# Six result buffers, a fetch lead that grows step by step, and 128 blank rows in a fused attention and expert kernel

## The chip, the cores and the metric

The kernel runs on one core of a Trainium2 chip. The metric is the device time of one execution in microseconds. The profile comes from one further execution, recorded instruction by instruction.

## The reference, cut to what matters

The input is an image tensor of 2 x 56 x 56 positions with 256 channels, all in 32-bit floats. Two layers are applied. The first is a neighbourhood attention with windows of 7 x 7. The second is a linear attention over the 3136 positions of each image, followed by a mixture of eight experts, of which each token uses the two with the highest gate value:

```python
x = x + _L0_conv_ref(_gn(x), ...)             # neighbourhood attention
t = _to_tokens(x)
t = t + _L1_attn_ref(_ln_t(t), ...)           # linear attention, a running sum over tokens
t = t + _L1_ffn_ref(_ln_t(t), ...)            # experts

def _L1_ffn_ref(x, gate_w, gate_b, W1, b1, W2, b2):
    probs = softmax(xf @ gate_w + gate_b)
    top2_vals, top2_idx = top_k(probs, 2)
    # for each expert: out += weight * (gelu(xf @ W1 + b1) @ W2 + b2)
```

An expert's matrices are 256 x 512 and 512 x 256. There are 6272 tokens and so 12544 pairs of token and expert.

## The kernel before, in words

**Stages.** Roughly the first third of the span is the first layer. The second layer then goes through the tokens in 13 steps of 256 tokens per image (`NS1 = 13`, the last step has 64). In step `s`, `attention(s)` is the main line of work; beside it run `before(s + 1)`, which prepares the projections of the next step, `route(s - 1)`, which gates the tokens of the step before, and some expert tiles. `together` advances these generators in proportion: each side line has a nominal count of turns (`n_route = 23` for the routing), and a `yield` in a generator ends one turn. After the last attention step comes a pass in which `route(12)` is the main line, and then the tail, in which only expert tiles are left. The program lists instructions in this order for each engine; the framework's own scheduler may still move an instruction within its engine's queue.

**Routing.** `route` computes for every token and each of its two experts a row number in a DRAM table `xs_d`, in which each expert owns a region of rows (DVE, ending with `rowi`, L1293). It then issues up to eight indirect DMAs from POOL (L1299) that scatter the normalized tokens, with their token numbers and gate values, to those rows.

**Expert tiles.** The rows of an expert are worked in tiles. 48 tiles are whole, with 256 rows, and 9 are half, with 128 rows; `order` mixes them, and from tile 41 on half and whole tiles alternate (half: 41, 43, 45, 47, 49, 51, 53, 55 and 56). A tile passes these places:

- `fetch(k)`: SP loads the rows `xg` (L1452) and the expert's weights and biases `wj` (L1461, 1154 KB). The buffers for both lie in pools of four (`FW = 4`): `fw` during the steps, and from the tail on `fw` and a second pool `tw` in turns of four tiles. `ask(k)` in `experts` lists the fetches of all tiles up to a lead, `use.ahead`, beyond the one being worked. The lead is 2 in the steps and 5 from the start of the tail.
- `gather(k)`: DVE takes the tokens' numbers `rowk` and gate values `cws` from the rows (pool `fs`, six buffers), PE transposes the rows (L1492), ACT copies them (L1496).
- `hidden(k)`: PE multiplies by the first matrix into `p_h` (L1507), ACT applies gelu into `hT` (L1514).
- `results(k)`: ACT writes gate value times bias into the result buffer `ye` (L1526, pool `fy`, four buffers of one tile each); PE multiplies by the second matrix into `p_y` (L1532); DVE multiplies by the gate value and adds into `ye` (L1539); POOL issues an indirect DMA with addition into the output for each 128 rows (L1542). Two tiles can hold the same token, so each addition waits until all additions of the tile before have landed:

```python
before_it = added[-1] if added else []
...
waits_for(add, *before_it)
```

**Blank rows.** Before the first fetch that can reach beyond an expert's last token, `blank()` (L1418) writes empty rows behind each of the eight regions from SP (L1427), so that the unused rows of an expert's last tile hold zero gate values.

Of the kernel before, what the change touches and what calls it, by code (L numbers as in the profile page):

```python
# [24 lines left out]
P = 128  # L25
# [24 lines left out]
NF = FF // P  # L50
# [6 lines left out]
SL = 256  # L57
# [9 lines left out]
FW = 4  # L67
# [24 lines left out]
def sure1(s):  # L92
    return max(0, -((NE * (SL - 1) - assigned(s)) // SL))
# [689 lines left out]
def layer1(tc, t, out, x1_d, xs_d, ident, load, K, plain, lx, last_row, lite):  # L783
# [12 lines left out]
    with ExitStack() as whole:  # L796
# [403 lines left out]
        def route(s):  # L1200
# [3 lines left out]
            for b in range(NB):  # L1204
                store = nc.gpsimd.dma_start(
                    out=out[b * L + s * B1 : b * L + s * B1 + W].rearrange("(j p) e -> p j e", p=T),
                    in_=x[:T, b, :nj, :],
# [70 lines left out]
            n = p2.tile([P, NB * NJ + 1, NE], F32, tag="n", name="n")  # L1278
# [15 lines left out]
                rowi[:T, :, :nt], rows, float(NE * RG), float(NE * RG + SL - 1), ALU.add, ALU.min  # L1294
            )
            yield
            for i in range(nt):
                for c in range(2):
                    put = nc.gpsimd.indirect_dma_start(  # L1299
                        out=xs_d[:, :],  # L1300
                        out_offset=bass.IndirectOffsetOnAxis(
                            ap=rowi[:T, c, i : i + 1].bitcast(U32), axis=0
                        ),
                        in_=xs[:T, i, :],
                        in_offset=None,
                    )
                    tc.declare_no_dep(put.ins, group="puts", reason="slots of other tokens")
                    tc.add_to_no_dep_group("puts", put.ins)
                    tc.add_to_no_dep_group(f"puts{s}", put.ins)
                    puts.setdefault(s, []).append(put)  # L1310
                    tc.declare_no_dep(put.ins, group="gets", reason="full tiles are not written again")
                yield
# [105 lines left out]
        def blank():  # L1418
            for e in range(NE):
                row = nc.values_load(  # L1420
                    behind_[0:1, e : e + 1],
                    engines=[mybir.EngineType.SP],
                    min_val=e * RG,
                    max_val=e * RG + NB * L,
                    skip_runtime_bounds_check_because="an expert has at most K.every token",
                )
                put = nc.sync.dma_start(  # L1427
                    out=xs_d[bass.ds(row, SL), :].rearrange("(u p) c -> p u c", p=P), in_=empty
                )
                tc.declare_no_dep(put.ins, group="puts", reason="slots behind the last token")  # L1430
                tc.declare_no_dep(put.ins, group="gets", reason="full tiles are not written again")
                tc.add_to_no_dep_group("puts", put.ins)
                tc.add_to_no_dep_group(f"puts{NS1}", put.ins)
                puts.setdefault(NS1, []).append(put)

        def fetch(k, pool):
            n = parts(k)
            if filled_at(k) == NS1 and NS1 not in puts:
                blank()
            known = "the lists hold rows of the regions and experts alone"  # L1440
            row, exp = (
                nc.values_load(
                    entry[order[k]][0:1, w, order[k] : order[k] + 1],
                    engines=[mybir.EngineType.SP],
                    min_val=0,
                    max_val=top,
                    skip_runtime_bounds_check_because=known,
                )
                for w, top in ((0, NE * RG), (1, NE - 1))
            )  # L1450
            xg = pool.tile([P, SL // P, ROW], F32, tag="xg", name="xg")
            get = nc.sync.dma_start(  # L1452
                out=xg[:, :n], in_=xs_d[bass.ds(row, n * P), :].rearrange("(u p) c -> p u c", p=P)
            )
            tc.add_to_no_dep_group("gets", get.ins)
            for earlier in range(filled_at(k) + 1):
                waits_for(get, *puts[earlier])
            for later in range(filled_at(k) + 1, NS1 + 1):
                tc.declare_no_dep(get.ins, group=f"puts{later}", reason="slots of later steps")
            wj = pool.tile([P, WJ], F32, tag="wj", name="wj")  # L1460
            nc.sync.dma_start(out=wj, in_=t["we"][bass.ds(exp, 1)].rearrange("o p c -> (o p) c"))  # L1461
            fetched[k] = xg, wj
# [97 lines left out]
        use = SimpleNamespace(ahead=2, asked=0, tail=None)  # L1560
        done = [0]

        def ask(k):
            while use.asked < min(k, NP):
                n = use.asked
                fetch(n, use.w if use.tail is None or (n - use.tail) // FW % 2 else tw)
                use.asked += 1

        def experts():
            for k in range(NP):  # L1570
                ask(k + use.ahead + 1)
                if k == 0:
                    made = gather(0, use.x, use.psum)
                    yield
                wj = fetched[k][1]
                hT = yield from hidden(made[0], wj, use.x, use.psum)
                if k + 1 < NP:
                    following = gather(k + 1, use.x, use.psum)
                    yield
                yield from results(k, hT, made, wj, use.x, use.psum)  # L1580
                made = following
                fetched.pop(k)
                done[0] = k + 1
                yield

        run = experts()

        def until(k):
            while done[0] < k:
                if next(run, 0) is None:  # L1590
                    yield

        def together(main, *others):
            going = [[gen, n, 0] for gen, n in others]
            n_main = main[1]
            made = 0
            for made, _ in enumerate(main[0], 1):
                for o in going:
                    while o[2] * n_main < made * o[1] and next(o[0], 0) is None:
                        o[2] += 1  # L1600
            for gen, _, _ in going:
                for _ in gen:
                    pass
            return made
# [4 lines left out]
        for _ in first:  # L1609
# [6 lines left out]
        empty = load(const, "empty1", [P, SL // P, ROW], t["empty"].rearrange("p (u c) -> p u c", u=SL // P))  # L1616
        nc.gpsimd.dma_start(
            out=xs_d[NE * RG : NE * RG + SL, :].rearrange("(u p) c -> p u c", p=P), in_=empty
# [7 lines left out]
        apart1 = const.tile([1, 1], F32, name="apart1")  # L1626
        nc.vector.tensor_reduce(apart1, pf, AX.X, ALU.max)
        nc.vector.tensor_single_scalar(plain, apart1, 0.0, ALU.is_equal)
        n_att, n_route, per_tile = 26, 23, NF + 1 + SL // P
        for s in range(NS1 + 1):  # L1630
            others = []
            if s == 0:
                others.append((beside_it, NT * NG + 1 - given))
            if s + 1 < NS1:
                others.append((before(s + 1) if s else second, n_before))
            if 0 < s < NS1:
                others.append((route(s - 1), n_route))
            upto_k = max(0, (sure1(s - 2) if s > 1 else 0) - use.ahead)
            n = upto_k - done[0]
            if n > 0:  # L1640
                others.append((until(upto_k), n * per_tile))
            if s < NS1:
                got = together((attention(s), n_att), *others)
                n_att = got if s == 0 else n_att
            else:
                together((route(s - 1), n_route), *others)
            if s + 2 < NS1:
                load_x(s + 2)
            if s == 0:
                beside.close()  # L1650
                lite.close()
                fs, fx, fy, fw = (
                    whole.enter_context(tc.tile_pool(name=n, bufs=k, reuse_waits="tile", side="right"))
                    for n, k in (("fs", 6), ("fx", 2), ("fy", 4), ("fw", FW))
                )
                ps_m = steps.enter_context(
                    tc.tile_pool(name="l_mm", bufs=8, space=PSUM, reuse_waits="tile")
                )
                use.x, use.w, use.psum = fx, fw, ps_m
# [7 lines left out]
        with (  # L1667
            tc.tile_pool(name="tw", bufs=FW, reuse_waits="tile") as tw,
            tc.tile_pool(name="t_ps", bufs=8, space=PSUM, reuse_waits="tile") as ps_t,
            tc.tile_pool(name="tx", bufs=3, reuse_waits="tile") as tx,  # L1670
        ):
            use.x, use.psum, use.ahead, use.tail = tx, ps_t, 5, use.asked
            for _ in run:
                pass

# [901 lines left out]
```

## Time and profile before

| | |
|---|---|
| median of 3 runs | 1396.23 us (1392.82 to 1402.47) |
| the profiled execution | 1395.47 us, span 1393.7 us |
| PE busy | 1249.2 us (90% of the span) |
| DVE, ACT, POOL busy | 788.7, 583.6, 469.3 us |
| mean granted TensorE clock | 0.945 |
| additions into the output (L1542) | 105, 1574 ns each on POOL, idle before them 357.9 us |

The span is the time from the first to the last instruction; 1.77 us of the execution lie outside it. Busy time of POOL at an indirect DMA is the time of the instruction, not of the transfer, which lands some microseconds later. A wait is put down to the event that the trace shows last before it.

### The profile page before, as it was taken

To read this page: it belongs to the slowest core of one execution; us is meant where nothing else is said; L and a number is where in the kernel's file an instruction comes from. 1 tells how busy PE (TensorE), PEld (TensorE's weight loads), DVE (VectorE), ACT (ScalarE), POOL (GpSimd) and SP (SyncE) were. 2 spreads that over 40 slices of the span, in tenths; PEclk is the share of its full clock that TensorE was granted. 3 is DMA by queue.
4 is the path that set the end of the run, shared out by engine and by line. 5 is a ranking of instruction groups with operands and counts; after the bars stand their busy time and mean duration, and the time that the engine had idled before them with its cause. 6 is when DMAs were issued, how large, how long until landed. Compare 5 with 4: busy or idle time off the path is not lost.

```text
span 1393.7 us, 29855 instructions
## 1 busy us (share of the span) xinstructions
PE 1249.2 (90%) x11566; PEld 907.3 (65%) x11566; DVE 788.7 (57%) x2680; ACT 583.6 (42%) x1053; POOL 469.3 (34%) x514
## 2 busy tenths in 40 slices
PE   1899889999989996887999999999999999698893
PEld 1567667677755754445576767676777788587783
DVE  6546555465786657757575666666574755341110
ACT  1443444444444242342554454454535454352341
POOL 0222222223341123133161625253534435452333
PEclk9999999999989697977999999999999999999997
DMA  8345443334431011032435536362726366579852
GB/s 288 90 122 152 121 145 112 116 107 120 130 119 41 25 40 48 18 103 66 173 106 154 163 103 181 93 201 74 196 75 177 93 169 187 173 218 342 276 111 31
DMA packets 101292, 183.21 MB, mean 131 GB/s; under 512 B 15587, under 2 KB 84707, under 8 KB 93845
## 3 DMA queue, kind: packets, MB, share of 16 engines
q1 hardware_dynamic: 69108, 128.96, 28.2%
q0 software_dynamic: 28864, 47.21, 14.8%
q10 hardware_dynamic: 3168, 5.05, 1.1%
q8 instruction: 93, 1.52, 0.5%
q14 instruction: 59, 0.48, 0.1%
HBM read 131.76 MB, written 49.39 MB: 130 GB/s over the span
## 4 chain that ended last, share of the span: by engine, by line
PE 43%; DVE 12%; DMA 4%; issue 3%; ACT 2%; POOL 1%; POOLq 0%; ACTq 0%; DVEq 0%; SPq 0%
PE p_y L1532 11%; PE p_h L1507 9%; PE p_qkv L929 8%; PE p_out L1182 4%; DMA out<-ye,rowk 3%; PE cx L1164 2%; PE p_u L951 2%; PE cx L1151 2%; PE p_sum L966 1%; DVE am L1113 1%; PE pt_x L901 1%; PE p_cf L1064 1%; PE pt_g L1492 1%; ACT wide L1054 1%; DMA out<-x_acc 1%
## 5 line engine op out<-in xcount | busy, mean ns | idle before, releaser
L1542 POOL DMA_INDIRECT out<-ye,rowk x105 | 165.3, 1574 | 357.9 <-DVE ye L1539 100.6
L1532 PE MATMUL p_y<-wj,hT 128*128 128x256 f32 x840 | 206.8, 392 | 25.7 <-ACT hT L1514 19.6
L1507 PE MATMUL p_h<-xT_g,wj 128*128 128x256 f32 (+1 forms) x912 | 209.7, 371 | 2.2 <-DVE ye L1539 1.2
L1532 PEld LDWEIGHTS p_y<-wj,hT 128*128 128x128 f32 x840 | 156.4, 195 | 56.3 <-ACT hT L1514 23.8
L394 ACT ACTIVATE ex<-ex 98x1024 f32<-98x1024 f32 x98 | 103.6, 1057 | 196.2 <-DVE ex L388 192.8
L1507 PEld LDWEIGHTS p_h<-xT_g,wj 128*128 128x128 f32 x912 | 155.4, 191 | 27.3 <-issue 6.0
L1514 ACT ACTIVATE hT<-p_h,wj 128x256 f32<-128x256 f32 (+1 forms) x228 | 99.5, 453 | 106.0 <-PE p_h L1507 105.0
L1539 DVE SCALAR_TENSOR_TENSOR ye<-p_y,cws,ye 128x256 f32<-128x256 f32 x105 | 50.4, 480 | 154.8 <-PE p_y L1532 154.7
L388 DVE TENSOR_TENSOR ex<-sc,bias 98x1024 f32<-98x1024 f32 (+1 forms) x112 | 120.1, 1082 | 27.7 <-PE sc L379 24.2
L379 PEld LDWEIGHTS sc<-qb,kc 64*98 64x98 f32 x1568 | 94.5, 168 | 51.1 <-issue 26.1
L379 PE MATMUL sc<-qb,kc 64*98 64x128 f32 x1568 | 118.3, 289 | 4.0 <-DVE am L1113 2.2
L1299 POOL DMA_INDIRECT xs_d<-xs,rowi x100 | 98.2, 982 | 70.2 <-DVE first L1341 31.4
L402 PE MATMUL po<-vw,ex 98*64 98x33 f32 x3136 | 116.3, 229 | 5.0 <-DMA vw<-v_d 2.7
L402 PEld LDWEIGHTS po<-vw,ex 98*64 98x64 f32 x3136 | 104.9, 143 | 22.8 <-ACT ex L394 4.2
L346 POOL TENSOR_TENSOR xo<-xo,xq 128x256 f32<-128x256 f32 x49 | 36.1, 736 | 226.9 <-DVE xo L340 212.2
L1526 ACT ACTIVATE ye<-wj,cws 128x256 f32<-128x256 f32 x105 | 50.2, 507 | 73.7 <-issue 31.1
L1137 POOL TENSOR_TENSOR zc<-z,blk 128x256 f32<-128x256 f32 x48 | 38.9, 923 | 115.0 <-DVE z L1135 107.0
L506 PE MATMUL pvv<-L_wvT,xs 128*112 128x256 f32 x224 | 61.1, 413 | 13.3 <-DVE top L498 13.3
L873 DVE BATCH_NORM_STATS2 st<-x_acc 128x6 f32<-128x256 f32 (+1 forms) x100 | 38.3, 412 | 51.9 <-DMA x_acc<-x_d 51.5
L1113 DVE TENSOR_TENSOR am<-sc,upto 128x512 f32<-128x512 f32 (+1 forms) x100 | 60.9, 670 | 7.3 <-PE sc L1104 7.2
L348 POOL DMA_DIRECT2D x_d<-xo x98 | 56.7, 580 | 16.6 <-POOL xo L346 14.6
L1176 ACT COPY cT<-cx 128x256 f32<-128x256 f32 (+1 forms) x50 | 18.3, 366 | 103.1 <-PE cx L1164 102.9
(261 smaller groups left out, 2150.0 us busy)
## 6 DMA issues: line engine op xcount, KB each, us to landing
wj<-in_we SPq DMA_DIRECT2D x57, 1154.0 KB
vw<-v_d SPq DMA_DIRECT2D x196, 101.1 KB
xg<-xs_d SPq DMA_DIRECT2D x48, 272.0 KB
v_d<-values POOLq DMA_DIRECT2D x28, 231.0 KB, 3.3
xq<-in_x SPq DMA_DIRECT2D x98, 64.0 KB
x_d<-xo POOLq DMA_DIRECT2D x98, 64.0 KB, 3.2
x_acc<-x_d SPq DMA_DIRECT2D x24, 256.0 KB
out<-x_acc POOLq DMA_DIRECT2D x24, 256.0 KB, 5.1
```

Of the source, the lines that this page charges most:

```text
L379: nc.tensor.matmul(at[p][:KN, b, k], lhsT=keys(i, j, k, b, rows, g), rhs=qb[rows, g, :, b, j * QN : (j + 1) * QN], start=True, stop=True,)
L388: nc.vector.tensor_tensor(ex[:KN, of], sc[:KN].rearrange("n p b k h q -> n p b (k h q)"), tables[kind][:KN, g, of].unsqueeze(2).to_broadca ...
L394: nc.scalar.activation(ex[:KN], ex[:KN], AF.Exp)
L402: nc.tensor.matmul(po[b * QN : (b + 1) * QN, hh, :], lhsT=ex[:KN, h // 2, b, k, h % 2, :], rhs=vw[:KN, b, k, hh * (HD + 1) : (hh + 1) * (H ...
L506: nc.tensor.matmul(ps, lhsT=xs[:, b, k, j * TT : (j + 1) * TT], rhs=wv[:, k, :], start=k == 0, stop=k == NG - 1,)
L929: nc.tensor.matmul(ps[:, :, :W], lhsT=w[:, kk, g * P : (g + 1) * P], rhs=xT[:, kk, :, :W], start=kk == 0, stop=kk == NG - 1,)
L1113: nc.vector.tensor_tensor(am[:T, h, :, :, :T].rearrange("p b g t -> p (b g) t"), sc[:T, :, :, :T].rearrange("p b g t -> p (b g) t"), K.upt ...
L1299: put = nc.gpsimd.indirect_dma_start(out=xs_d[:, :], out_offset=bass.IndirectOffsetOnAxis(ap=rowi[:T, c, i : i + 1].bitcast(U32), axis=0), ...
L1507: nc.tensor.matmul(ph, lhsT=w1[:, k, f * P : (f + 1) * P], rhs=xT[:, k, :], start=k == 0, stop=k == NG - 1,)
L1514: nc.scalar.activation(hT[:, f, :], ph, AF.Gelu, bias=b1[:, f : f + 1])
L1532: nc.tensor.matmul(py, lhsT=hT[:, f, u * P : (u + 1) * P], rhs=w2[:, f, :], start=f == 0, stop=f == NF - 1,)
L1542: add = nc.gpsimd.indirect_dma_start(out=out[:, :], out_offset=bass.IndirectOffsetOnAxis(ap=rowk[:, u : u + 1].bitcast(U32), axis=0), in_= ...
```

## The change

Five edits, in four groups:

1. The result pool `fy` has six buffers instead of four, and `fs`, which holds the row numbers and gate values that go with them, eight instead of six.
2. The lead `use.ahead` is not set to 5 when the tail begins. It grows by one at every odd tile of the tail, from 2, until it is 5.
3. `blank()` writes 128 rows behind each expert instead of 256. A last tile with at most 128 rows is a half tile, so no tile reaches further than that.
4. `route` has one more `yield`, between the row numbers and the scatters, and its nominal count of turns is 24 instead of 23.

```diff
@@ route
                 rowi[:T, :, :nt], rows, float(NE * RG), float(NE * RG + SL - 1), ALU.add, ALU.min
             )
             yield
+            yield
             for i in range(nt):
@@ blank
                 put = nc.sync.dma_start(
-                    out=xs_d[bass.ds(row, SL), :].rearrange("(u p) c -> p u c", p=P), in_=empty
+                    out=xs_d[bass.ds(row, P), :], in_=empty[:, 0, :]
                 )
@@ experts
             for k in range(NP):
+                if use.tail is not None and k % 2 and use.ahead < 5:
+                    use.ahead += 1
                 ask(k + use.ahead + 1)
@@ layer1
-        n_att, n_route, per_tile = 26, 23, NF + 1 + SL // P
+        n_att, n_route, per_tile = 26, 24, NF + 1 + SL // P
...
-                    for n, k in (("fs", 6), ("fx", 2), ("fy", 4), ("fw", FW))
+                    for n, k in (("fs", 8), ("fx", 2), ("fy", 6), ("fw", FW))
...
-            use.x, use.psum, use.ahead, use.tail = tx, ps_t, 5, use.asked
+            use.x, use.psum, use.tail = tx, ps_t, use.asked
```

## The prediction

> **What bounds the kernel now.** I read the page's slices first, then the span cut into stretches, then the waits, and last the time line of POOL and the end of the chain. The slices say that PE is full from about 660 us to 1188 us (18.7 to 20.0 us busy in nearly every 20 us). No edit can give much there. The last fifth is different. Cut into stretches (us, then busy time of PE, PEld, DVE, ACT, POOL, then granted clock, DMA share, GB/s):
>
> ```profile
> 1209.00:1221.00 12.00, 1.96 (x9) 1.25 (x8) 0.00 (x0) 1.70 (x5) 3.17 (x3) 0.66 0.58 167
> 1221.00:1257.00 36.00, 36.00 (x177) 30.29 (x176) 16.62 (x106) 16.05 (x35) 18.40 (x14) 0.97 0.82 222
> 1257.00:1300.00 43.00, 36.09 (x176) 30.77 (x174) 5.37 (x27) 12.26 (x31) 10.80 (x7) 0.92 1.01 365
> 1300.00:1335.00 35.00, 32.25 (x167) 27.46 (x168) 5.61 (x29) 14.07 (x39) 13.80 (x9) 0.95 0.81 228
> 1335.00:1373.00 38.00, 37.52 (x210) 32.76 (x208) 6.94 (x33) 15.44 (x43) 15.54 (x11) 1.00 0.34 49
> ```
>
> PE stands for 10 us at 1209, loses 7 and 3 us in the next two stretches that have holes, and the DMA engines are full from 1257 to 1300. The waits of that part name two queues, ACT and POOL:
>
> ```profile
> ACT ye L1526 <- issue: 31.1, 6, 11.4
> ACT ye L1526 <- DMA out<-ye,rowk: 12.7, 6, 7.2
> POOL out L1542 <- DMA out<-ye,rowk: 81.8, 19, 8.5
> ```
>
> "Issue" hides what it was; the time line of POOL shows it:
>
> ```profile
> 1206.81 0.96 POOL L1299 DMA_INDIRECT xs_d<-xs,rowi  x1 [0.30 <-issue]
> 1208.07 1.60 POOL L1542 DMA_INDIRECT out<-ye,rowk  x1 [0.30 <-issue]
> 1209.98 1.57 POOL L1542 DMA_INDIRECT out<-ye,rowk  x1 [0.30 <-issue]
> 1220.07 1.55 POOL L1542 DMA_INDIRECT out<-ye,rowk  x1 [8.52 <-DMA out<-ye,rowk]
> ...
> 1271.70 1.54 POOL L1542 DMA_INDIRECT out<-ye,rowk  x1 [0.30 <-DVE own_e L1479]
> 1281.73 1.54 POOL L1542 DMA_INDIRECT out<-ye,rowk  x1 [8.49 <-DMA out<-ye,rowk]
> ...
> 1338.80 1.54 POOL L1542 DMA_INDIRECT out<-ye,rowk  x1 [3.68 <-DMA out<-ye,rowk]
> 1340.64 1.54 POOL L1542 DMA_INDIRECT out<-ye,rowk  x1 [0.30 <-issue]
> 1345.25 1.54 POOL L1542 DMA_INDIRECT out<-ye,rowk  x1 [3.07 <-DMA out<-ye,rowk]
> 1349.65 1.54 POOL L1542 DMA_INDIRECT out<-ye,rowk  x1 [2.85 <-DMA out<-ye,rowk]
> ```
>
> Counted back from the last tile, 56, the pair at 1208.07 and 1209.98 is tile 32, 1220.07 is 33, 1271.70 is the second of 39, 1281.73 is 40, 1345.25 is the half tile 49. An ACT bias copy of tile 36 (L1526, 1219.30) needs one of four buffers, the one of tile 32, so it started when the additions of 32 had landed, and two gelus of tile 34 stood behind it in ACT's queue; PE needed them. So ACT is stopped by a full set of buffers, and the buffers are full because the additions go tile by tile. This chain of additions also sets the end:
>
> ```profile
> 1373.29 3.75 DMA out<-ye,rowk
> 1377.82 3.54 DMA out<-ye,rowk
> 1382.39 1.26 POOL out L1542
> ```
>
> PE's last product ends near 1372.6; the rest is additions. Undisturbed, a whole tile costs the chain 6.45 us (1338.80 to 1345.25) and a half tile 4.40 us. PE needs 7.35 us for a whole tile (3.46 + 3.45 + 0.44) and about 3.7 us for a half one. A pair is thus 10.85 us of chain against 11.1 us of PE: nearly even. From 1251.18 (tile 37) to 1382.11 (tile 56) the chain took 130.9 us; 11 whole and 8 half tiles undisturbed are 71.0 + 35.2 = 106.2. The excess of 24.7 us is slow landing: steps of 11.3, 11.9, 10.8 us for the whole tiles 38 to 40 and 8.2 for the half tile 41, all while the DMA share was 1.
>
> **What the Trainium skill says.** "DMA: Bandwidth & Descriptors", section "Issuing engines are not separate DMA queues", says that DMAs from SP and POOL run on the same 16 engines and interleave. Its section "SWDGE vs HWDGE vs iDMA" adds that inside an engine the queues of the two kinds are served in turn. The trace agrees: an addition lands in 3.8 us (median after 1335) and in 8.8 us (median from 1257 to 1300, weight fetches going). So an addition should pay for every microsecond in which fetches are under way, whether they come in one burst or in two. "Perfetto Trace Analysis", section "DMA Instruction — SWDGE (GPSIMD)", says that the profiled end of such an instruction is when the descriptors are written, not when data has moved; here 1.54 us of POOL against 3.5 to 10.1 us to landing.
>
> **The change, part by part.**
>
> *Six result buffers.* A bias copy then needs the additions of two tiles earlier, 10.85 us of chain or more. The 10.0 us hole at 1209 goes, and with it the slow clock behind it (12 products in 4.24 us instead of 2.6): PE gains 11.7 us. In the burst it gains again, since holes of 3.5, 1.4 and 2.9 us before `p_y` are of the same kind. But PE is not what ends last. What the chain of additions gets from an earlier PE is only the time in which it waited for results and not for a landing. With 4.6 us from a second addition to the next tile: tile 35 waited 0.5 us (1233.44 against 1228.32 + 4.6), tile 36 1.9 us, tile 37 3.0 us (its results at 1249.9 and four scatters ahead of it). Sum 5.4 us. The four scatters of step 12 (4 x 1.22 us on POOL) stay; they can lie in the 3 us for which POOL waits for a landing, and the rest, 1.9 us, may stay on the chain. Bounds 3.5 and 5.4 us; I take 5.4, because a chain that never runs dry leaves such a gap at every tile. What is late next: the chain itself, from tile 32 to 56.
>
> *Fetch lead.* SP runs nothing but fetches there. Listing a fetch later in the program puts nothing in front of it: the order on SP stays 41, 42, 43 and so on, and what holds a fetch is a buffer (`p_y` of eight tiles before) or an earlier transfer, as the waits of SP in the tail say (up to 10.4 us for `p_y`, 1.7 to 3.1 us for an earlier `wj`). So I cost it at nothing. If the framework does hold the fetches back, the burst of 41 to 46 at 1257 to 1268 is spread; the bytes stay the same and so, by the section on queues, does most of the excess. Bounds: a gain of 12 us (half the excess) and a loss of 3 us (one tile's weights, 1154 KB at 390 GB/s, late once).
>
> *Blank rows.* Eight DMAs of 136 KB instead of 272 KB. SP's issue time (10.02 us for all eight, the register loads included) hardly changes. 1.09 MB less at 372 to 390 GB/s is 2.9 us less of full DMA engines, and the excess was 18.4 us in the 42 us from tile 38 to tile 41's successor, 0.44 per us: 1.3 us off the chain. Bounds 0 and 2.9.
>
> *The turn in route.* With the old count, one routing turn falls on about one attention turn (24 turns in some 66 us), and there are 20 of them; the scatters begin at the 16th, now at the 17th of 21. They come up to 2.7 us later. They issue eight indirect DMAs (0.98 us each), and behind them in POOL's queue stand `zc` (L1137) and the next additions; SP's fetches of the next rows wait for them to land. POOL waited about 5 us for `rowi` before each block (31.4 us in 7 times), which shrinks. PE was full there, and rows fetched at 1045.08 were transposed no earlier than 1058.59, so a delay of 2.7 us is covered by 9 us. At step 12, where attention has only ten turns, most of the routing runs in one piece, so its eight scatters stay ahead of tile 32's addition. I cost it at 0; bounds -3 (a gain) and +3 us.
>
> Sum: 5.4 + 0 + 1.3 + 0 = 6.7 us off the profiled execution's 1395.47, which is 1388.8. That execution lies 0.8 us under the median of the runs, less than their spread, and I add nothing for it.
>
> **Rivals.** *The additions land faster.* If thinner fetching halves the excess, 12.4 us more go: 1395.5 - 6.7 - 12.4 = 1376.4. For it: tiles 42 and 44 landed in about 4 us between two fetches, so gaps in the fetching do help. Against: the order and the buffers of the fetches stay. At most the whole excess goes, and tile 32 is added before the scatters (results at 1198.8, issued at 1208.07: 9.3 us): 1395.5 - 5.4 - 24.7 - 9.3 = 1356.
>
> *Bias copies run further ahead and block ACT* (the slower side). The framework put tile 36's copy ahead of tile 34's gelu while four buffers allowed it. With six it may put a copy three tiles ahead. It then waits for that tile's weights: the copy of 41 ahead of the gelu of 38 (1250.5) would wait for weights issued at 1257.74 and landed near 1262, 11.5 us in which PE stands, with 1.6 us of slow clock after it. The hole at 1209 comes back in the same way, so nothing is won there: 1395.5 + 13.1 - 1.3 = 1407.3. It decides as soon as a copy stands more than two tiles ahead of the gelu behind it. Against it: in the tail every copy stands one tile ahead, tied to its gate values.
>
> **How the numbers follow.** Forecast 0.46, faster landing 0.36, blocked ACT 0.18. The likeliest is 1388.8. Its own range is 1382 to 1394. The range from 1368 to 1406 leaves out the best end of the first rival and the worse half of the second, under 0.2 in all. About 1% (14 us) is what a measurement of this kernel can tell from no change: faster by more takes most of the first rival and a little of the forecast, 0.38; slower by more the worse part of the second, 0.12; the rest is 0.50.
>
> **What would show it.** Right: no hole in PE near 1209; ACT's waits for `ye` well under 43.8 us; PE's last product more than 13 us before the last addition; POOL waiting for a landing before nearly every tile from 32 to 56; additions still near 9 us under full DMA. Wrong: additions near 4 to 5 us in the burst (first rival), ACT waiting for `wj` or again for `ye` (second), or a PE that ends last, which would mean that the chain of additions was never the bound.

## The result, and the profile after

The kernel after takes 1406.9 us in the median of 17 runs (1401.76 to 1414.02), the kernel before 1397.93 us beside it (17 runs). The ratio is 1.0059, with a 95% interval from 1.0044 to 1.0074: slower by some 8 us, where 6.7 us less were forecast. The profiled execution took 1409.65 us (span 1407.9, mean granted clock 0.936), 14.2 us more than the one before. The two profiles thus lie further apart than the medians, and what is read from them is the place of a loss sooner than its exact size. Of the 14.2 us, 7.7 are there when tile 32 is first added (1208.07 before, 1215.79 after); the other 6.5 lie in the chain of additions from there to tile 56 (174.0 and 180.5 us).

From the added `yield` on, line numbers of the kernel after are one higher: L1543 is L1542 of the kernel before. The tail of the kernel after in stretches (columns: us, busy time of PE, PEld, DVE, ACT, POOL, then clock, DMA share, GB/s):

```profile
1217.00:1229.00 12.00, 12.00 (x65) 9.73 (x63) 1.45 (x3) 3.76 (x10) 4.07 (x4) 1.00 0.90 293
1229.00:1265.00 36.00, 34.49 (x167) 29.25 (x165) 15.87 (x105) 15.08 (x31) 15.38 (x12) 1.00 0.60 142
1265.00:1281.00 16.00, 6.34 (x22) 5.12 (x23) 0.86 (x5) 2.23 (x6) 4.81 (x4) 0.68 0.98 347
1281.00:1309.00 28.00, 24.62 (x145) 22.05 (x143) 5.04 (x28) 10.22 (x27) 6.17 (x4) 1.00 1.05 380
```

The hole that stood at 1209 is gone: PE is busy in all 12 us of the first line. A new one stands in the third, 9.7 us of 16, with the clock at 0.68. The waits of that part (1188 to 1408; us in total, how often, the longest) and ScalarE's time line say who made it:

```profile
POOL out L1543 <- DMA out<-ye,rowk: 99.1, 21, 8.7
ACT ye L1527 <- issue: 16.8, 5, 5.1
ACT ye L1527 <- DMA wj<-in_we: 16.5, 1, 16.5
ACT ye L1527 <- DMA out<-ye,rowk: 11.4, 6, 5.4
```

```profile
1257.09 0.59 ACT L1497 COPY xT_g<-pt_g 128x512 f32<-128x512 f32 x1
1274.17 0.51 ACT L1527 ACTIVATE ye<-wj,cws 128x256 f32<-128x256 f32 x1 [16.49 <-DMA wj<-in_we]
1274.59 1.55 ACT L1515 ACTIVATE hT<-p_h,wj 128x256 f32<-128x256 f32 x4
```

The bias copy of tile 41 stands in ScalarE's queue in front of the four gelus of tile 40. In the kernel before the same copy stood there too (1264.55), but waited only 3.66 us, for numbers from VectorE (`own_e`, worked out from the tile's rows). Now it waits for its weights. These are late because SyncE asks for the rows of tile 41 first, and waits 14.1 us for the last scatters to land. The scatters stand on POOL behind the additions of tile 36:

```profile
SPq L1453 <- DMA xs_d<-xs,rowi: 14.1, 1, 14.1
```

```profile
1248.64 1.54 POOL L1543 DMA_INDIRECT out<-ye,rowk  x1 [8.71 <-DMA out<-ye,rowk]
...
1254.98 1.54 POOL L1543 DMA_INDIRECT out<-ye,rowk  x1 [2.95 <-DMA out<-ye,rowk]
1256.83 1.54 POOL L1543 DMA_INDIRECT out<-ye,rowk  x1 [0.30 <-issue]
1258.67 0.94 POOL L1300 DMA_INDIRECT xs_d<-xs,rowi  x1 [0.30 <-issue]
```

But this hole is not what the additions waited for. The first additions of tiles 38 to 41 found their results ready and waited for the tile before to land:

```profile
1275.36 1.54 POOL L1543 DMA_INDIRECT out<-ye,rowk  x1 [8.33 <-DMA out<-ye,rowk]
...
1287.12 1.54 POOL L1543 DMA_INDIRECT out<-ye,rowk  x1 [8.36 <-DMA out<-ye,rowk]
...
1298.24 1.54 POOL L1543 DMA_INDIRECT out<-ye,rowk  x1 [7.73 <-DMA out<-ye,rowk]
...
1309.91 1.54 POOL L1543 DMA_INDIRECT out<-ye,rowk  x1 [8.28 <-DMA out<-ye,rowk]
```

From tile 37 (1263.56) to tile 42 (1317.27) the chain took 53.7 us, 49.5 before. From tile 32 to 37, where the forecast had its gain, it took 47.8 us in place of 43.1. The steps from 35 to 36 and from 36 to 37 did become shorter, by 2.0 and 0.8 us. But the step from 33 to 34 grew from 6.4 to 9.9 us, with a wait of 6.5 us for results from VectorE, and the step from 34 to 35 from 7.0 to 12.1 us, with the wait of 8.71 us for a landing shown above. No run looks into these two. From 42 to 56 the chain took 79.0 us in place of 81.4.

The end is still additions: from 1358.82 the chain that ended last goes from one landing to the next, and the steps are as long as before:

```profile
1380.90 3.73 DMA out<-ye,rowk
1387.22 3.79 DMA out<-ye,rowk
1391.79 3.74 DMA out<-ye,rowk
```

**A loss before the tail.** 7.7 of the 14.2 us are lost before 1200 us, where I had seen nothing to lose. The first scatter of each step on POOL serves as a mark. The first mark stands at 536.86 before and at 540.05 after; in all the traces of this case it lies anywhere from 535.0 to 541.0, so these 3.2 us are not put down to the change. In the kernel before two later marks stand at 708.16 and 769.51, 61.4 us apart; in the kernel after at 710.52 and 777.27, 66.8 us apart. The steps after that take 66 us in both. So the step of 66.8 us is where the change can have lost 5.4 us. Inside that step VectorE's time line of the kernel after holds this:

```profile
725.46 0.16 DVE L862 SCALAR_TENSOR_TENSOR root<-root_a,root 128x4 f32<-128x4 f32 x1
725.65 4.70 DVE L860 TENSOR_TENSOR root_a<-root 128x4 f32<-128x4 f32 x1
730.38 0.16 DVE L861 SCALAR_TENSOR_TENSOR root_a<-root_a,ve 128x4 f32<-128x4 f32 x1
```

An operation on 128 x 4 numbers that takes 0.16 us in the lines around it took 4.70 us. GpSimd at the same time:

```profile
725.82 2.13 POOL L1205 DMA_DIRECT2D out<-x_acc  x2
727.34 2.98 POOL L914 TENSOR_TENSOR x_acc<-x_acc,bo 128x1024 f32<-128x1024 f32 x1
```

The small operation ends at 730.35, GpSimd's addition of a bias row to the residual tile (L914, in `before`) at 730.32. L860 to L862 are the steps of the inverse root for the normalization in `route`; ScalarE's normalization waits for them (4.9 us at 731.62), two gelus stand behind it, and PE is busy for 2.99 us of the 6 from 728 to 734. In the kernel before, the same chain of small operations ends just before GpSimd begins:

```profile
723.76 0.16 DVE L862 SCALAR_TENSOR_TENSOR root<-root_a,root 128x4 f32<-128x4 f32 x1
723.96 0.16 DVE L881 SCALAR_TENSOR_TENSOR nm<-mv,root 128x4 f32<-128x4 f32 x1
```

```profile
724.17 2.13 POOL L1205 DMA_DIRECT2D out<-x_acc  x2
725.69 2.99 POOL L914 TENSOR_TENSOR x_acc<-x_acc,bo 128x1024 f32<-128x1024 f32 x1
```

724.12 against 724.17: a margin of 0.05 us. Unstopped, VectorE's chain takes 2.6 us from its first step (L878) on. In the kernel before it begins 2.66 us before GpSimd's stores, in the kernel after 1.36 us before them. The other traces say the same. In 13 of the traces of this case the addition L914 has its old place. In the four of them with the turn the chain begins between 1.36 us before the stores and 0.51 us after them, and all four show a stop of 4.0 to 4.7 us. In eight of the nine without the turn it begins 2.6 to 2.8 us before them, and there is no stop. The ninth (six buffers without weight fetches in the tail, which differs from the kernel before only in the result buffers until then) has 1.95 us, and L860 is stopped for 4.69 us at 730.22. The step takes 65.2 to 66.8 us in the five with the stop and 61.4 to 63.9 in the eight without. In the list of GpSimd's instructions the turn alone changes the order in this step only: both `zc` products now stand before the first scatter, and three scatters in place of four before the next addition into the output. How this makes the chain and the stores meet was not followed further.

The Trainium skill names a mechanism: "SBUF — State Buffer", section "Who interferes with whom", says that VectorE and GpSimd share one pair of ports to SBUF, that an operation of VectorE with two inputs in SBUF, or one in a mode that uses both ports, contends with a GpSimd operation that reads SBUF, and that whoever is second is blocked until the other's whole instruction is done. The trace agrees that the small operation ends with GpSimd's addition. It does not agree in who is second: VectorE's operation begins, on record, 1.69 us before the addition (725.65 and 727.34), so the block of 4.70 us is longer than the 2.98 us of the addition. It spans the stores in front of it too. The third and fourth groups of runs below test whether the addition is the cause.

### The profile page after: what moved, and what is told of

Same layout as the page of the kernel before. It is cut to its first block, busy times and chain, and to the rows that moved or that the text cites. A ratio compares the mean times of both kernels' runs of the same rounds, so it can differ in the third digit from the quotient of the medians.

```text
span 1407.9 us, 29872 instructions
## 1 busy us (share of the span) xinstructions
PE 1254.3 (89%) x11566; PEld 911.4 (65%) x11566; DVE 789.4 (56%) x2680; ACT 583.1 (41%) x1053; POOL 468.6 (33%) x514
## 4 chain that ended last, share of the span: by engine, by line
PE 41%; DVE 11%; DMA 6%; ACT 2%; issue 2%; POOL 2%; POOLq 0%; ACTq 0%; DVEq 0%
PE p_y L1533 9%; PE p_qkv L929 8%; PE p_h L1508 8%; DMA out<-ye,rowk 6%; PE p_out L1182 4%; PE cx L1164 2%; PE cx L1151 2%; PE p_u L951 2%; PE p_sum L966 1%; PE pt_x L901 1%; DVE am L1113 1%; POOL out L1543 1%; DVE root_a L860 1%; PE p_cf L1064 1%; PE pt_g L1493 1%
## 5 line engine op out<-in xcount | busy, mean ns | idle before, releaser
L1543 POOL DMA_INDIRECT out<-ye,rowk x105 | 165.3, 1574 | 368.1 <-DMA out<-ye,rowk 109.1
L1533 PEld LDWEIGHTS p_y<-wj,hT 128*128 128x128 f32 x840 | 155.4, 194 | 48.7 <-ACT hT L1515 16.5
L1113 DVE TENSOR_TENSOR am<-sc,upto 128x512 f32<-128x512 f32 (+1 forms) x100 | 60.8, 669 | 6.3 <-PE sc L1104 6.3
L1164 PE MATMUL cx<-am,kp 128*32 128x128 f32 (+1 forms) x800 | 54.7, 309 | 4.7 <-DVE am L1113 4.7
```

The lines of the kernel that those rows point to most:

```text
L1113: nc.vector.tensor_tensor(am[:T, h, :, :, :T].rearrange("p b g t -> p (b g) t"), sc[:T, :, :, :T].rearrange("p b g t -> p (b g) t"), K.upt ...
L1164: nc.tensor.matmul(cx[hp, g, :T], lhsT=kp[:T, b, g, hp], rhs=am[:T, h, b, g, :T], start=False, stop=True,)
L1533: nc.tensor.matmul(py, lhsT=hT[:, f, u * P : (u + 1) * P], rhs=w2[:, f, :], start=f == 0, stop=f == NF - 1,)
L1543: add = nc.gpsimd.indirect_dma_start(out=out[:, :], out_offset=bass.IndirectOffsetOnAxis(ap=rowk[:, u : u + 1].bitcast(U32), axis=0), in_= ...
```

## The experiments

The runs were made in four groups on different chips, on which the kernel before took 1444.46, 1398.93, 1399.96 and 1446.5 us. Each ratio is to the kernel before beside it, and across groups only ratios and stretches of single traces are compared.

**Each part alone.** The six buffers:

```diff
-  (("fs", 6), ("fx", 2), ("fy", 4), ("fw", FW))
+  (("fs", 8), ("fx", 2), ("fy", 6), ("fw", FW))
```

> Six result buffers alone (fs 8, fy 6), everything else as before. The instructions stand in the same order on every engine as in the kernel before; only waits of bias copies differ. Theory A (the chain of additions sets the end, PE's hole near 1209 us goes and the chain never runs dry): 3 to 6 us faster. Theory B (the rows of tile 41 wait for the last step's scatters, and these stand in POOL's queue behind the additions of tile 36, so a PE that is 11 us ahead stands later instead, when the bias copy of tile 41 waits for weights in front of tile 40's gelu): within 3 us of before, or up to 7 us slower, with a wait of ACT for wj of over 10 us near 1260 us.

The lead:

```diff
+                if use.tail is not None and k % 2 and use.ahead < 5:
+                    use.ahead += 1
...
-            use.x, use.psum, use.ahead, use.tail = tx, ps_t, 5, use.asked
+            use.x, use.psum, use.tail = tx, ps_t, use.asked
```

> The growing lead alone. The list of instructions and of their waits comes out the same on all engines as before, so both theories expect no difference: within 2 us. It serves as a measure of how far two equal programs differ.

The blank rows:

```diff
-                    out=xs_d[bass.ds(row, SL), :].rearrange("(u p) c -> p u c", p=P), in_=empty
+                    out=xs_d[bass.ds(row, P), :], in_=empty[:, 0, :]
```

> 128 blank rows alone. Theory A: 1 to 3 us faster (2.9 us less of full DMA engines). Theory B: the fetch of tile 41 waits for blank rows in the kernel before (SP's fetch at 1256.9 us, scatters done at 1250.2 us), so it comes about 3 us earlier, but additions set the end: 0 to 3 us faster.

The turn:

```diff
+            yield
...
-        n_att, n_route, per_tile = 26, 23, NF + 1 + SL // P
+        n_att, n_route, per_tile = 26, 24, NF + 1 + SL // P
```

> The extra turn in route alone (count 24). Theory A: no difference, within 3 us. Theory B': the order of ACT, DVE and PE in the steps changes, with bias copies moved ahead of other copies, and one step near 727 us loses some 5 us while ACT waits for nm; the profile of the changed kernel is 5.4 us later there than the one before: 4 to 7 us slower, all of it before 780 us.

| alone | ratio | interval |
|---|---|---|
| six buffers | 1.0028 | 1.0003 to 1.0053 |
| lead | 1.0000 | 0.9976 to 1.0023 |
| 128 blank rows | 0.9985 | 0.9962 to 1.0007 |
| turn | 1.0027 | 1.0007 to 1.0048 |

The sum is +0.0040, against +0.0059 for all together: the two agree within the intervals. The lead does nothing: with it alone the list of instructions on each engine is the same, in the same order. Buffers and turn each cost some 4 us, with intervals that begin at 0.4 and 1.0 us. With the buffers alone no copy on ScalarE waits for weights in the tail, where theory B had asked for over 10 us, and the additions from tile 37 to 42 take 53.3 us all the same. With the turn alone the step from 711 us on took 65.8 us; in the other three 61.8 to 62.4.

**Three edits of the kernel after, and one of the kernel before.** The turn taken out again (the diff just shown, turned round); the bias copies tied behind their own tile's last gelu (`use.gelu`, set in `hidden`); the last step's routing first; and, on the kernel before, no weight fetches in the tail:

```diff
@@ results: tied copies
-                nc.scalar.activation(y[:, u, :], wj[:, WJ - C :], AF.Identity, scale=cws[:, u : u + 1])
+                behind(nc.scalar.activation(y[:, u, :], ...), use.gelu)
@@ the last step: routing first
-                together((route(s - 1), n_route), *others)
+                list(route(s - 1)) + [list(gen) for gen, _ in others]
@@ fetch: no weights in the tail
+            if use.tail is not None:
+                wj = fetched[use.tail - 1][1]
```

> The kernel after with the added turn taken out again (six buffers, the growing lead and 128 blank rows stay). Theory T, the turn's own loss: the turn alone cost 1.0027 and stretched the step from about 711 to 777 us by 4 to 5 us; without it that step takes 61 to 63 us again, and the ratio to the kernel before falls from 1.0059 to 1.0010 to 1.0025 (buffers 1.0028 and blank rows 0.9985 remain). Rival I, the parts hurt each other in the tail and the turn is innocent: the ratio stays at 1.005 to 1.007, and the loss stands behind the mark at 1200 us.

1.0012 (0.9995 to 1.0030), and the step takes 61.9 us: the turn is worth 0.0047 of the 0.0059. Theory T holds.

> The kernel after with one edit: each bias copy stands in ScalarE's queue behind the last gelu of its own tile, so that it can no longer stand in front of gelus of the tile before. Both theories expect the 16 us wait of the bias copy for the weights of tile 41, and TensorE's hole there, to go. Theory C, the serial additions set the end: the first addition of tile 37 to that of tile 56 still takes 130 to 134 us, and the ratio to the kernel before falls by 0.003 at most, to 1.003 to 1.006. Rival A, the blocked ScalarE queue sets the end: the end comes about 10 us earlier than in the kernel after, ratio 0.997 to 1.000.

1.0115 (1.0088 to 1.0143), outside both expectations. The wait for the weights is gone and nothing is won, which speaks against rival A. It does not rule it out by itself, since the edit brings a wait of its own. Tiles 37 to 56 were added in 137.7 us (132.7 in the kernel after), and VectorE now waits for the copies:

```profile
DVE ye L1540 <- PE p_y L1533: 56.9, 25, 6.0
DVE ye L1540 <- ACT ye L1527: 50.7, 9, 8.8
```

The profiled execution (1408.99 us) is near this kernel's shortest, so it does not show where all of the further loss of 0.0056 lies.

> The kernel after with one edit: in the last step the routing runs to its end before the remaining expert work is begun, so the last four scatters stand on GpSimd in front of the additions of tiles 35 and 36. The slots of tile 41 are then asked for some 10 us earlier and the wait for its weights shrinks below 8 us. Theory C (the additions' chain sets the end, from tile 32 on): the chain from 32 to 56 keeps its length of 173 to 181 us and the end comes 0 to 4 us earlier than in the kernel after: ratio 1.003 to 1.006. Rival A (late fetches behind the scatters set the end): 8 to 12 us earlier, ratio 0.997 to 1.000. Third way: TensorE idles while the routing runs alone, and the ratio rises above 1.007.

1.0009 (0.9983 to 1.0035): 0.0050 less than the kernel after, about 7 us. That is more than theory C allowed and at the edge of rival A. The additions from tile 32 to 56 took 170.2 us in place of 180.5. The rows of tile 41 were asked for at 1245.16 in place of 1264.90, and the fetches behind them met other additions. The chain still sets the end, but its length is not fixed, as theory C had it; I take it that it depends on which additions the fetches meet; this run does not show it.

> The kernel before with one edit that leaves work out: the tiles asked for in the tail fetch no weights and use those of the last tile fetched before the tail. Theory C with contention (an addition lands late because weight fetches fill the DMA engines): the first addition of tile 37 to that of tile 56 shrinks from 131 us to 104 to 112 us, the medians of an addition's landing fall to about 4 us, and the ratio is 0.978 to 0.986. Rival N (the additions take this long by themselves, or the engines' pace spaces them): the stretch stays above 122 us and the ratio at 0.990 or above.

0.9865 (0.9843 to 0.9886), some 19 us, just above the range that theory C gave. Tiles 37 to 56 were added in 110.5 us in place of 130.9, so 20.4 us of the excess of 24.7 go with the weight fetches. A part of them may be results that come earlier, since PE now never stands in the stretch shown. The stretch from tile 37 to 42, in the kernel before and in this one:

```profile
1251.18:1300.68 49.50, 41.91 (x205) 35.90 (x203) 6.57 (x31) 15.50 (x40) 13.97 (x9) 0.93 1.01 352
```

```profile
1250.86:1284.44 33.58, 33.58 (x182) 30.05 (x182) 5.90 (x28) 14.78 (x38) 13.96 (x10) 1.00 0.65 138
```

Rival N falls.

**GpSimd's addition out of VectorE's way.** L914 is queued behind the two `zc` products that follow it on POOL, about 5 us later; nothing needs its result before the next step's attention:

```diff
@@ before
-            nc.gpsimd.tensor_tensor(x[:T, :, :nj, :], ..., ALU.add)
+            use.later.append(lambda: nc.gpsimd.tensor_tensor(x[:T, :, :nj, :], ..., ALU.add))
@@ attention, after the zc products
+                while use.later:
+                    behind(use.later.pop()(), use.zc)
```

> The kernel before with one instruction moved: GpSimd's addition of a bias row to the residual tile (x_acc, 128 x 1024, about 2.95 us) is queued behind the two zc products that follow it, some 5 us later. Theory P (that addition, when it meets VectorE's chain of small steps for the inverse root, holds VectorE up for 3.4 to 4.7 us, and with it ScalarE's gelus and TensorE): where the kernel before shows no such stall after 700 us (a run of about 1398 us), the move brings nothing, ratio 0.998 to 1.002; where it shows one in each step from about 770 us on (a run of about 1444 us, steps of 72 to 75 us in place of 66), the steps come down to 66 us and the ratio to 0.965 to 0.975. Rival Q (the stalls are only where a delay shows, not its source): the steps keep their length, ratio 0.997 to 1.003 in both cases; worse than 1.005 if the later place delays the next step.

> The kernel after with the same instruction moved behind the two zc products. Theory P: the stall of 4.7 us that the turn brought to the step at 711 to 777 us goes, that step takes 61 to 63 us, and the ratio to the kernel before falls from 1.0059 to 1.000 to 1.002 where the kernel before runs at about 1398 us; where it runs at about 1444 us, the ratio is 0.967 to 0.977. Rival Q (the turn costs its 4 to 5 us by another order of TensorE's work): the step keeps 65 to 67 us and the ratio stays at 1.004 to 1.007.

The kernel before with the move: 0.9916 (0.9883 to 0.9949). The kernel after with it: 0.9961 (0.9944 to 0.9978), so the move took 0.0098, about 14 us, off the kernel after. In neither trace does a small operation of the chain take over 1.2 us. The step of 66.8 us takes 63.5, and the move is worth more than theory P had said, in both kernels. I had overlooked that the chain was stopped in earlier steps too: in the kernel before for 2.95, 2.34 and 2.22 us at 551, 605 and 660 us. From the mark near 537 us to that near 708 us the two kernels took 171.3 and 170.5 us, with the move 162.1 and 161.3, so 9.2 us come from there in each. In the step after the mark at 708 the kernel after gains 3.2 us more, and the kernel before, which had no stop there, loses 3.0 (61.4 to 64.3 us), which I had not expected and have not explained.

> The kernel before with one edit: in the last step the routing runs to its end before the remaining expert work is begun, so that the last four scatters stand on GpSimd in front of the additions of tiles 35 and 36. In the kernel after the same edit took 0.0050 off the ratio. If late weights for tile 41 and fetches that meet the additions cost the kernel before as well: 0.994 to 0.998. If it only mends what the six buffers and the turn had brought: 0.999 to 1.002.

> The kernel before with the six buffers (rowk, cws and own_e eight) and with the routing of the last step first. Compared with the routing alone (run beside it). Theory W (six buffers cost 0.003 because the bias copy of tile 41 now stands in ScalarE's queue waiting for weights that come late): with the slots asked for earlier that wait is under 5 us, and the two kernels differ by less than 0.0015, or the buffers win. Rival V (the buffers' cost lies elsewhere): this kernel is 0.002 to 0.004 above the routing alone.

Routing first on the kernel before: 0.9983 (0.9965 to 1.0001), in neither of the two ranges; a gain of about 2 us at best is likely. With six buffers as well: 0.9999 (0.9974 to 1.0024). The difference of 0.0016 decides neither for W nor for V, but the traces do: no bias copy waits for weights any more, and tiles 37 to 42 still took 43.9 us with six buffers and 38.2 with four. As in the run with the buffers alone, that wait is not what they cost, so theory W falls.

**What the buffers cost, and a version that uses what was found.** The diffs are those above, combined.

> The kernel before with GpSimd's addition moved behind the zc products, and with six buffers (rowk, cws, own_e eight). The move alone gave 0.9916. Theory B (the remainder is the six buffers': tiles 37 to 42 are added more slowly because more fetches meet them): 0.994 to 0.997, and the first addition of tile 37 to that of tile 42 takes 51 us or more where the move alone had 49.2. Rival T (the turn's): 0.990 to 0.993.

> The kernel before with GpSimd's addition moved behind the zc products, and with the turn. The turn's loss was the stall of VectorE alone (theory P): 0.990 to 0.993, the same as the move alone within the interval. Rival T (the turn costs something beside the stall, for instance by its other order of ScalarE's copies): 0.994 to 0.997.

> The kernel before with six buffers, and with one edit that leaves work out: the tiles asked for in the tail fetch no weights and use those of the last tile fetched before the tail. With four buffers this gave 0.9865. Theory B (the buffers' cost comes from fetches that meet the additions): no cost is left, 0.984 to 0.9875, and tiles 37 to 42 are added in 33 to 35 us. Rival V (it lies elsewhere): 0.988 to 0.992.

> The kernel before with three edits: GpSimd's addition moved behind the zc products, the last step's routing first, and 128 blank rows in place of 256. By themselves they gave 0.9916, 0.9983 and 0.9985: if they add up, 0.988 to 0.990, faster than both kernels; if the routing first merely takes up what the move has gained, 0.990 to 0.993.

| kernel | ratio | interval |
|---|---|---|
| move and six buffers | 0.9844 | 0.9801 to 0.9886 |
| move and turn | 0.9813 | 0.9768 to 0.9859 |
| six buffers, no weight fetches in the tail | 0.9875 | 0.9848 to 0.9902 |
| move, routing first, 128 blank rows | 0.9853 | 0.9810 to 0.9896 |

The ratios of the three kernels with the move are lower than expected, since the ranges took the ratio of another chip. The kernel before takes longer on this chip (1446.5 us), as it had in the first group (1444.46 us), and there the stop is in more steps. On this chip the run without weight fetches, where the addition has its old place, shows stops of 2.8 to 4.5 us in five steps from 805 to 1100 us, and steps of 72 to 74 us. In the first group a trace with the same instructions as the kernel before (the lead alone) has steps of 73 to 75 us after 774 us and the stop in five of them, for instance:

```profile
872.67 4.47 DVE L860 TENSOR_TENSOR root_a<-root 128x4 f32<-128x4 f32 x1
```

```profile
872.59 2.13 POOL L1205 DMA_DIRECT2D out<-x_acc  x2
874.15 2.96 POOL L914 TENSOR_TENSOR x_acc<-x_acc,bo 128x1024 f32<-128x1024 f32 x1
```

872.67 + 4.47 is 877.14, 874.15 + 2.96 is 877.11. With the move the stops are gone and the steps take 69 to 71 us. Why not 66, as on the other chips, is open. The run with the move and six buffers also separates the stores from the addition: here the stores, without the addition behind them, overlap the chain, and no small step of it is longer than 0.20 us. (In the whole trace 49 of these small operations lie beside such stores; the longest took 0.53 us.)

```profile
790.72 1.69 POOL L1207 DMA_DIRECT2D out<-x_acc  x2
```

```profile
790.83 0.17 DVE L856 TENSOR_SCALAR root<-root_a 128x4 int32<-128x4 int32 x1
791.04 0.16 DVE L860 TENSOR_TENSOR root_a<-root 128x4 f32<-128x4 f32 x1
791.23 0.16 DVE L861 SCALAR_TENSOR_TENSOR root_a<-root_a,ve 128x4 f32<-128x4 f32 x1
```

So the stores alone do not stop the chain, and the addition is needed for it. Why the stop begins before the addition's recorded start stays open. Once the addition is moved, the turn no longer stretches the step after the mark near 703 us: 62.0 us without it (move and six buffers) and 61.5 with it on this chip, 64.3 and 63.5 on that of the third group. That is what theory P asked for. The ratios 0.9813 and 0.9844 overlap and agree with it, but the move alone did not run on this chip.

The buffers' cost shows in the additions. From tile 37 to tile 42 they took 48.2 to 49.7 us in the six traces with four buffers (before, lead, blank rows, turn, move, move and turn) and 52.3 to 54.4 in the five with six (after, buffers alone, after without the turn, after with the move, move and six buffers). The trace of the kernel after for that stretch:

```profile
1263.56:1317.27 53.71, 38.16 (x190) 32.66 (x189) 6.59 (x36) 15.28 (x41) 13.97 (x10) 0.87 1.00 357
```

The DMA engines are full there, as in the kernel before (352 GB/s), so a longer stretch moves more bytes in any case. The number of fetches says more. When tile 42 is first added, SyncE has issued 54 weight fetches in each of the five traces and 52 in each of the six; with the tied copies it has issued 56, and the stretch took 55.7 us. SyncE's fetches wait for PE to be done with an earlier tile's weights (76.5 us in all from 1188 us on before, 57.8 after), and with more result buffers PE gets there sooner. Where the time goes differs. With all edits it is the step of tile 37 that grows (11.8 us in place of 7.4), as the weights of tile 41 are asked for 2.2 us after its first addition and not 6.6 us after it; with the buffers alone it is the step of tile 41 (10.7 us, 8.2 in the kernel before). Some of it is given back later: the whole stretch from 37 to 56 took 133.1 us on average in the five traces and 130.5 in the six. Without weight fetches in the tail, six buffers (110.6 us) and four (110.5 us) are the same, and tiles 37 to 42 took 34.1 and 33.6 us. Theory B agrees with all of this. That it is the two more fetches which make the landings late is argued from these counts; no run changed the fetches alone with six buffers in place, other than to take all of them away. The size, 2.6 us in single traces against 0.0028 (4 us) in the medians, is known only roughly.

The version with the three edits is faster than the kernel before (0.9853), and by the ratios also than the kernel after, which did not run beside it. Whether it is faster than the move alone is not settled, since the two ran on different chips.

## Why the prediction was wrong

- **The hole at 1209**: right. It went, and PE began the products of tile 40 3.2 us earlier than before although it had come 7.7 us later into the tail, so about 11 us were won on PE where 11.7 had been worked out.
- **What the chain of additions gets from it**, -5.4 us: this step failed. The chain sets the end, as forecast (the chain that ended last is made of landings). But of the three gaps that were to close, those before 36 and 37 gave 2.8 us together, and the chain from 32 to 37 still took 47.8 us in place of 43.1, that from 37 to 56 132.7 in place of 130.9. I took an earlier PE as a source of earlier results only. An earlier PE also fetches earlier, and in the traces the additions from 37 to 42 then land later; that the fetches are the reason is argued above, and why the steps to 34 and 35 grew is open. The alone-run of the buffers gave +0.0028, a loss of about 4 us (0.4 to 7.7), in place of the gain.
- **Why the landing is slow**: right, in its cause. Without weight fetches 20.4 of the 24.7 us of excess go, as one would expect from what was cited of "DMA: Bandwidth & Descriptors" in the Trainium skill ahead of the result: the DMAs of SP and POOL run on the same engines and interleave.
- **Rival "bias copies block ACT"**: half right. ScalarE did stand 16.5 us for a copy that waits for late weights. It was not a copy put further ahead: on ScalarE the buffers alone leave the order as it was. And it is not what set the end: tiles 38 to 41 waited for landings and not for results while PE stood, the buffers alone cost their 4 us without such a wait, and the tied copies, which took it away, made the kernel slower. The agreement of its 1407.3 us with the measured time is chance.
- **The turn**, 0 with bounds of 3 us either way: this step failed, and it is the greater part. I asked only whether the scatters' delay was covered by work of PE. I did not ask what the shifted GpSimd queue would newly run beside. GpSimd's addition now met VectorE's chain of small steps and stopped it for 4.7 us in one step, which took 66.8 us in place of 61.4. The run without the turn gave 0.0047 back (6.6 us), and with the addition moved out of the way the step is as short with the turn as without.
- **The blank rows**, -1.3 us: the run gave 0.9985 (-2.1 us), with no change inside the interval; in keeping with it, not shown.
- **The lead**, 0: right.
- **The signs**: no hole near 1209, a last product of PE 21 us before the last addition (1375.40 and 1396.28) and waits for a landing before most tiles were as named for "right". None of them looked at the steps before the tail.

Put together, by the single runs: turn +0.0027 (in the kernel after +0.0047), buffers +0.0028, blank rows -0.0015, lead 0.

## What to carry to other kernels

A change that only shifts work on GpSimd by a microsecond is not free because PE is busy: look what VectorE runs beside it, and in the list of single instructions look for a small one that takes many times its usual time, since such a stop shows as a long instruction and not as a wait of VectorE. A long GpSimd operation on SBUF operands is better queued where VectorE is idle or works from PSUM. In the kernel before with the move, the addition runs from 724.10 to 726.45 while VectorE waits for other data until 734.05; in the kernel before, VectorE's products with an operand in PSUM (`am`, L1113) took 0.68 us each beside it, the median of them all. A margin of 0.05 us between two engines can be lost by any edit or on another chip. And when a buffer is added to free an engine, follow the freed engine to the transfers that it starts earlier, and ask whom these slow down.

## What the hardware showed that was not expected

- A VectorE step of 0.16 us took 2.2 to 4.7 us when it met GpSimd's addition, and ended within 0.04 us of it in the cases named above. It was not only operations with two inputs in SBUF: a tensor-scalar step with one (L853) took 4.45 us in the run with the lead alone.
- The block could be longer than the recorded blocking instruction: up to 4.7 us for 2.96 to 2.98 us where GpSimd's stores ran directly ahead of it, though stores alone stopped nothing.
- The same list of instructions met the block after 700 us in no step in one profile (the kernel before) and in five steps in another on another chip (the lead alone). On another such chip the steps with the move took some 70 us in place of 72 to 74 us, so the block is at most about half of what sets them apart from 66 us.
- An indirect DMA with addition landed much later beside other traffic: 3.7 to 3.9 us to land at the quiet end, and steps of 11 to 12 us for a whole tile while weights were fetched at 350 to 380 GB/s, against 6.4 us.
